# Four graph layers on one core: another order of the middle layers' work, X0's numbers on GpSimd, the last sums tile by tile

## The chip, the core and the metric

The kernel runs on one core of a Trainium2 chip. The time is that of one execution on the device in microseconds (us), the median of several runs. Engines are called as in the profile: PE (TensorE matmul), PEld (its weight load), DVE (VectorE), ACT (ScalarE), POOL (GpSimd), SP (SyncE, which issues the DMAs here).

## The reference

`x` is 3327 x 64, `adj` a 3327 x 3327 matrix of zeros and ones (about 0.5% ones). Four layers follow each other, each on the normalized input:

```python
h = jnp.maximum(_layernorm(x, axis=-1), 0.0)
x = x + layer(h, adj, ...)          # layers 0, 1, 2, 3

# layers 0 and 3, hyperbolic attention (layer 3 with c = 1 / r**2)
left, right = x_tan @ att_W[:D] + att_b, x_tan @ att_W[D:]      # x_tan = logmap0(x)
adj_att = sigmoid(left + right.T) * adj
x_local = logmap(x[:, None, :], x[None, :, :], C)
support_t = einsum('ij,ijd->id', adj_att, x_local)
return proj(expmap(x, support_t, C), C)

# layer 1, decay by rank among a row's neighbours
mask = (adj != 0); rank = cumsum(mask, axis=1); deg = rank[:, -1:]
k = minimum(deg, 100); pos = rank - (deg - k)
w = mask * where(pos > 0, 0.5 ** (k - pos), 0)
return w @ (h @ weight) + bias

# layer 2, sums over neighbours without the diagonal, and GRU cells
node_support = concat([(A > 0) @ h, (A < 0) @ h], axis=1)       # A = adj - its diagonal
edge_output = gru_cell(node_support, h, ...)
edge_support = softmax attention of A, times A, @ (h @ W_gat)
node_output = gru_cell(edge_support, h, ...)
return d[:, None] * edge_output + d[:, None] * node_output      # d = diagonal of adj
```

## The kernel before, in words

The nodes are padded to 3328, which is T = 26 tiles of 128 (P). The features D are 64. `X` holds all nodes as 128 x 26 x 64 in SBUF; half of it is 128 x 832 elements (`HALVES`).

**Hyperbolic layers (0 and 3).** A preparation (from L395) computes per node the factors that the pairwise logarithm needs. Its parts bear on the change: `of_x0` (L454), seven DVE operations of 128x26 that compute `x0` and split it into three fp16 parts; `of_e` (L463) and `of_f` (L467), which lay these parts out in the fp16 tile `Xe`; `to_columns16` (L478), which transposes 26 tiles of `Xp` or `Xe` by PE into PSUM tiles of four and has ACT and DVE in turn copy them out as XT and XE; `keep_busy` (L494), matmuls whose result nobody reads, 4 (L499) and 6 (L531); `of_left` (L514), which spreads `left` over the partitions; and small per-node numbers (L538 to L544). The operations on ACT, DVE, PE and POOL stand here in the order in which the code writes them. Then 104 steps follow (four chunks of columns, 1024 or 768 wide, by 26 tiles of rows). A step has two matmul pairs on PE (L588, L589), a Sigmoid on ACT (L575), a product with adjacency on POOL (L577), a Square on ACT (L595), two passes on DVE (L600, L601) and sums on PE (L610, L618). An epilogue (L698 to L796) computes per-node factors `ah` and `am` in some 60 operations of 128x26 and adds `ah * Xr + am * M` to X: per half of X a product (L793) and a sum (L794) for each of the two terms, where for the last term ACT has already made the product (`extra`, L786). This epilogue is not ordered by hand; a scheduler places its operations.

**Layer 1, decay** (`plain_decay`, L1273). The adjacency is read in 52 quarter tiles of 128x1664. For each, DVE makes an fp8 mask (L1326, 128x1664) and counts its zeros (`same`, L1248), PE counts ranks by triangular matrices (L1333), ACT turns them into weights by Exp (L1339), and PE sums (L1350). Its own layernorm (`norm_relu`, L123 to L146) and the product with the weight stand after the first two masks and ahead of the loop (L1386 to L1426). For 13 of the 52 quarters (`LATE`) the count of zeros is put off to layer 2.

**Layer 2, GAT** (`plain_gat`, L1431). PE sums over the masks kept from layer 1, in 26 steps (`b` from 25 to 0, L1518) of 16 matmuls each. In every second step DVE does one of the 13 late zero counts, for which the adjacency quarter is loaded again into a pool of 3 buffers (L1451). A table `todo` (L1510) puts other work behind certain steps: the transposes of h (`turn`), the degrees less the diagonal (`degrees`, L1488) and their inverse (`inverse`, L1497). After the steps `take` (L1536 to L1539) brings the sums from PSUM by ACT (L1538) and DVE (L1539), and two GRU cells follow in eight units: products on PE (L1546 to L1558), gates on ACT (L1565), `nn` on DVE (L1571, L1572), Tanh on ACT (L1575), the state on DVE (L1582 to L1586), and at the end the sum into X (L1613, L1614).

In the manually ordered pools, engine queues keep the order of the code. ACT has function tables: `table_of(F)` (L119) uses a function once on a spare element, so that its table is loaded at that place.

Of the kernel before, what the change touches and what calls it, by code (L numbers as in the profile page):

```python
# [9 lines left out]
F32 = mybir.dt.float32  # L10
# [36 lines left out]
def tile_gnn4(ctx: ExitStack, tc: tile.TileContext, x, adjT, att0, b0, w1, bias1, w_gat, a_gat,  # L47
# [274 lines left out]
    def hyperbolic_series(r, params, ok, masks=None, done=None):  # L322
# [18 lines left out]
        with ExitStack() as st:  # L341
# [53 lines left out]
            with tc.tile_pool(name="hsp", bufs=1) as tp, tc.tile_pool(name="hsps", bufs=2, space=PSUM) as ps, \  # L395
                    tc.manual_schedule(engines={mybir.EngineType.Activation, mybir.EngineType.DVE,
                                                mybir.EngineType.PE, mybir.EngineType.Pool}):
                Xe = tp.tile([P, T, KE + 9], F16, name="Xe")
# [11 lines left out]
                H, R, sq, sr = [tp.tile([P, T, D], F32, name=n) for n in ("H", "R", "sq", "sr")]  # L410
# [43 lines left out]
                def of_x0():  # L454
                    V.scalar_tensor_tensor(x0, x2, 1.0, ia, op0=OP.add, op1=OP.mult)
                    V.tensor_scalar(x0s, x0, SX, None, op0=OP.mult)
                    V.tensor_copy(p0[:, :, 0], x0s)
                    V.tensor_sub(rest, x0s, p0[:, :, 0])
                    V.tensor_copy(p0[:, :, 1], rest)
                    V.tensor_sub(rest, rest, p0[:, :, 1])  # L460
                    V.tensor_copy(p0[:, :, 2], rest)

                def of_e():  # L463
                    for k, src in ((0, h0.to_broadcast([P, T, 3])), (3, m0.to_broadcast([P, T, 2])), (5, l0)):
                        V.tensor_copy(E[:, :, k:k + src.shape[-1]], src)

                def of_f():  # L467
                    for k, src in ((0, p0), (3, hm0), (5, h0)):
                        V.tensor_scalar(Fe[:, :, k:k + src.shape[-1]], src, -1.0, None, op0=OP.mult)
                    G.tensor_copy(F, Fe)  # L470
# [7 lines left out]
                def to_columns16(dst, src, rows, odd, between=()):  # L478
                    between = list(between)
                    for t0 in range(0, T, 4):  # L480
                        n = min(4, T - t0)
                        pt = ps.tile([P, 4 * P], F16, name="pt", bufs=4)
                        for k in range(n):
                            PE.transpose(pt[:rows, k * P:(k + 1) * P], src[:, t0 + k, :], ident_h)  # L484
                        if t0 // 4 % 2 == odd:
                            V.tensor_copy(dst[:, t0 * P:(t0 + n) * P], pt[:rows, :n * P])
                        else:
                            A.activation(dst[:, t0 * P:(t0 + n) * P], pt[:rows, :n * P], AF.Copy)
                        if between:
                            between.pop(0)()  # L490

                junk, pe = [ps.tile([P, W], F32, name=n, bufs=1) for n in ("junk", "pe")]

                def keep_busy(n):  # L494

                    for _ in range(n):
                        PE.matmul(junk, ident_h, hi[:, :8, :], start=True, stop=True)

                keep_busy(4)  # L499
                to_columns16(XT, Xp[:, :, :2 * D], P, 1,  # L500
                             (of_x0, of_e, of_f, lambda: V.tensor_copy(Xe[:, :, :D], hi), of_z))
                columns(chunks[0])

# [8 lines left out]
                c = chunks[0]  # L512

                def of_left():  # L514

                    for o, to in ((0, junk), (1, pe)):
                        for i in range(c[1]):
                            t = o * HT + c[0] + i
                            PE.matmul(to[:, i * P:(i + 1) * P], left[:, t:t + 1].to_broadcast([P, P]), ident,
                                      start=True, stop=True)  # L520
                    V.tensor_copy(leftB[c][:, 0, :], junk[:, :c[1] * P])
                    A.activation(leftB[c][:, 1, :], pe[:, :c[1] * P], AF.Copy)

                to_columns16(XE, Xe, KE + 9, 0, (lambda: None, of_left))
                for o in range(2):
                    pt = ps.tile([P, 4 * P], F16, name="pt", bufs=4)
                    for i in range(c[1]):
                        PE.transpose(pt[:KE, i * P:(i + 1) * P], Xp[:, o * HT + c[0] + i, D:], ident_h)
                    V.tensor_copy(XF[c][:, o, :], pt[:KE, :c[1] * P])
                PE.transpose(pe[:T, :P], left, ident)  # L530
                keep_busy(6)  # L531
                A.activation(LT, pe[:T, :P], AF.Copy)
                nc.sync.dma_start(left_row, LT)
                V.tensor_copy(X0[:, :, 0], x0)
                V.scalar_tensor_tensor(good, x2, X2_MIN, nodes, op0=OP.is_ge, op1=OP.mult)
                V.reduce_sum(ok, good, axis=AX.X)
# [7 lines left out]
                V.tensor_scalar(small["bh"], ax, 0.5, isqc, op0=OP.mult, op1=OP.mult)  # L544

# [143 lines left out]
            with tc.tile_pool(name="hse", bufs=1) as tp:  # L689
# [43 lines left out]
                else:  # L733
# [8 lines left out]
                    V.tensor_mul(th, th, ti)  # L742
# [44 lines left out]
                for ts in HALVES:  # L787
                    for a, b in ((Xr, ah), (M, am)):
                        if ts is last and a is M:
                            prod = extra  # L790
                        else:
                            prod = tp.tile([P, T // 2, D], F32, name="prod", bufs=2)
                            V.tensor_mul(prod, a[:, ts, :], b[:, ts, None].to_broadcast([P, T // 2, D]))  # L793
                        V.tensor_add(X[:, ts, :], X[:, ts, :], prod)  # L794
                    if done is not None:
                        done(ts)  # L796
# [476 lines left out]
    def plain_decay(masks, zo, deg, wt, bias, gru, ball_of_r):  # L1273
# [11 lines left out]
        with ExitStack() as st:  # L1285
# [24 lines left out]
            with tc.tile_pool(name="pdacc", bufs=1, space=PSUM) as pa, tc.manual_schedule(  # L1310
# [20 lines left out]
                def counts(k, o, w):  # L1331
                    for h in range(2):
                        PE.matmul(cnt[o][:, h, :BK], w, cols(k, o, h), start=w is after and steps[k][1] == T - 1,  # L1333
                                  stop=True, skip_group_check=True)
# [30 lines left out]

                K_ = len(steps)
                make_mask(0)
                make_mask(1)
# [15 lines left out]
                for o in range(2):  # L1384
                    cnt[o] = pa.tile([P, 2, 512], F32, name=f"cnt{o}")
                for k in range(K_ + 2):  # L1386
                    c, b = steps[min(max(k, 0), K_ - 1)]
                    if 0 <= k < K_:
                        counts(k, 0, after)
                        weights(k, 0)  # L1390
                    if 0 <= k - 1 < K_:
                        counts(k - 1, 1, rest)
                        if steps[k - 1][1] == 0:
                            degrees(steps[k - 1][0], 1)
                    if 0 <= k < K_:
                        counts(k, 1, after)
                        weights(k, 1)
# [4 lines left out]
                    if 0 <= k < K_:  # L1402
                        counts(k, 0, rest)
                        if b == 0:
                            degrees(c, 0)
# [4 lines left out]
                    if k == 1:  # L1410
                        late()
# [19 lines left out]
    def plain_gat(masks, zo, deg, first, wg, gru):  # L1431
# [8 lines left out]
        with ExitStack() as st:  # L1440
# [10 lines left out]
            wk = st.enter_context(tc.tile_pool(name="pgl", bufs=3))  # L1451
# [4 lines left out]
            with tc.tile_pool(name="pgp", bufs=1) as tp, tc.tile_pool(name="pgacc", bufs=1, space=PSUM) as pa, \  # L1456
# [4 lines left out]

                hn = tp.tile([P, T, D], F32, name="hn")
# [25 lines left out]
                def degrees(k):  # L1488

                    cs = slice(k * BK, (k + 1) * BK)  # L1490
                    dg = bank(6 + k % 2)[:, :BK]
                    for o in range(2):
                        PE.matmul(dg[o * D:(o + 1) * D, :], ones_bf[:, :D],
                                  diag[:, o * HP + k * BK:o * HP + (k + 1) * BK], start=True, stop=True)
                    V.tensor_sub(deg[:, cs], deg[:, cs], dg)

                def inverse():  # L1497
# [8 lines left out]
                    table_of(AF.Sigmoid, r0[:, :1])  # L1506
                    V.scalar_tensor_tensor(deg, deg, -1.0, r0, op0=OP.mult, op1=OP.mult)
                    V.scalar_tensor_tensor(deg, deg, 2.0, r0, op0=OP.add, op1=OP.mult)

                todo = {T - 4: lambda: turn(0), T - 6: lambda: degrees(0), T - 8: lambda: turn(4),  # L1510
                        T - 9: lambda: degrees(1), T - 11: lambda: turn(8), T - 12: lambda: degrees(2),
                        T - 14: lambda: turn(12), T - 15: lambda: degrees(3), T - 17: inverse}
                for b in range(T - 1, -1, -1):
# [9 lines left out]
                    if b % 2 == 0:  # L1523
                        same = wk.tile([P, 2, CW], BF, name="same", bufs=1)
                        k = LATE[(T - 1 - b) // 2]
                        zeros(same, late.pop(0), zo[:, k:k + 1])


# [173 lines left out]
```

## Time and profile before

| | us |
|---|---|
| median of 3 runs (lowest, highest) | 819.15 (817.87, 821.02) |
| profiled execution, its time | 818.34 |
| its span | 816.6 |

The mean granted clock of PE was 0.924 in it. Busy share of the span: DVE 87%, PE 81%, ACT 71%, POOL 51%. The stages in the trace, from the span's start, are:

| stage | from, to (us) |
|---|---|
| layer 0: preparation; loop; epilogue | 0 to 36; 36 to 266; 267 to 284 |
| layer 1: norm; loop | 284 to 298; 298 to 428 |
| layer 2: norm; loop over masks; GRU cells and sum | 428 to 443; 443 to 486; 486 to 531 |
| layer 3: preparation; loop; epilogue | 531 to 561; 561 to 790; 791 to 811 |

In a line of a timeline the columns are: start, duration, engine, line of the code, operation, output and input by their names and shapes, count, and in square brackets the idle time just before on this engine and what ended it. "x2" with 2.08 us is two instructions in a row. Starts of successive lines can lie closer than the duration of one: operations overlap on an engine, and their pitch is what a sum needs. In a line of windows the numbers after the length are busy times of PE, PEld, DVE, ACT and POOL with counts, the mean clock, the DMA share and GB/s.

### The profile page before, as it was taken

What the parts mean: (1) busy time and instruction counts of PE and PEld (TensorE: products, weight loads), DVE (VectorE), ACT (ScalarE), POOL (GpSimd) and SP (SyncE); (2) the same over time, 40 slices, a digit from 0 to 9 for tenths busy, and PEclk for the clock granted to TensorE, in tenths of its full rate; (3) what the DMA queues carried; (4) which work ended last, traced back from release to release, by engine and by line L of the source; (5) the groups of instructions that cost most, each with busy time, mean ns of one, the idle gap of its engine ahead of it and who ended that gap; (6) DMA issues with size and microseconds to landing.
All of it is one profiled execution on the core that took longest, in us unless ns stands there. A gap on an engine that the chain in (4) does not pass through costs nothing. (4 is left out here: it accounts for less than half of the span.)

```text
span 816.6 us, 11802 instructions
## 1 busy us (share of the span) xinstructions
PE 659.8 (81%) x4215; PEld 252.1 (31%) x4215; DVE 709.1 (87%) x985; ACT 576.2 (71%) x729; POOL 416.1 (51%) x296
## 2 busy tenths in 40 slices
PE   0799999999999049989993995427999999999960
PEld 0522233333332024435441651214222333333320
DVE  6789999989998899998967567996899999999976
ACT  2678888878886367777782575255888888888862
POOL 2299988989987050003120000004687777787730
PEclk9989999999999569999996997757999999999995
DMA  3567676776664739998913541001001001000001
GB/s 75 164 203 219 205 212 184 205 213 196 196 189 120 292 131 327 372 379 298 367 36 132 187 151 50 1 4 45 1 1 34 1 1 36 1 1 2 1 2 46
DMA packets 57621, 107.84 MB, mean 132 GB/s; under 512 B 8752, under 2 KB 33488, under 8 KB 57552
## 3 DMA queue, kind: packets, MB, share of 16 engines
q1 hardware_dynamic: 53200, 106.97, 40.5%
q10 hardware_dynamic: 4352, 0.02, 0.3%
q8 instruction: 35, 0.57, 0.3%
q14 instruction: 34, 0.28, 0.1%
HBM read 103.72 MB, written 0.88 MB: 128 GB/s over the span
## 5 line engine op out<-in xcount | busy, mean ns | idle before, releaser
L595 ACT ACTIVATE y<-slot,shift_c 128x768 f32<-128x768 f32 (+1 forms) x208 | 197.4, 949 | 68.4 <-ACT sig L575 48.6
L601 DVE TENSOR_TENSOR sig<-slot,sig 128x768 f32<-128x768 f32 (+1 forms) x208 | 213.2, 1025 | 23.3 <-POOL sig L577 2.1
L600 DVE SCALAR_TENSOR_TENSOR slot<-y,slot 128x768 f32<-128x768 f32 (+1 forms) x208 | 212.1, 1020 | 9.1 <-ACT y L595 9.0
L577 POOL TENSOR_TENSOR sig<-adj,sig 128x768 f32<-128x768 f32 (+1 forms) x104 | 201.9, 1962 | 28.1 <-ACT sig L575 26.0
L575 ACT ACTIVATE sig<-leftB,right 128x768 f32<-128x768 f32 (+1 forms) x208 | 204.1, 981 | 3.5 <-DVE bh L544 3.5
L577 POOL TENSOR_TENSOR sig<-mask,sig 128x768 f32<-128x768 fp8e4 (+1 forms) x104 | 174.6, 1680 | 61.6 <-ACT sig L575 57.6
L610 PE MATMUL slot<-sig,Xr 128*64 128x384 f32 (+1 forms) x832 | 188.3, 541 | 16.8 <-DVE sig L601 16.8
L588 PE MATMUL slot<-XC,XT 128*128 128x384 f16 (+1 forms) x416 | 142.9, 344 | 5.2 <-DVE sig L601 3.5
L589 PE MATMUL slot<-XF,XE 73*128 73x384 f16 (+1 forms) x416 | 142.0, 341 | 0.0
L1339 ACT ACTIVATE w<-cnt,ebias 128x832 bf16<-128x832 f32 x104 | 93.7, 950 | 30.7 <-PE cnt L1333 30.7
L1248 DVE TENSOR_SCALAR_CACHE_REDUCE same<-adj 128x1664 bf16<-128x1664 f32 x52 | 97.5, 1876 | 3.6 <-DMA adj<-in 3.4
L618 PE MATMUL slot<-sig,X 128*32 128x384 f32 (+1 forms) x832 | 96.0, 533 | 0.0
L610 PEld LDWEIGHTS slot<-sig,Xr 128*64 128x64 f32 x832 | 43.1, 135 | 122.5 <-DVE sig L601 83.4
L1333 PE MATMUL cnt<-mask,after 128*128 128x416 fp8e4 x208 | 54.8, 347 | 22.7 <-DVE mask L1326 19.8
L588 PEld LDWEIGHTS <-XT 128*128 128x128 f16 x416 | 40.8, 98 | 96.1 <-issue 70.7
L191 POOL TENSOR_TENSOR mask<-mask,offdiag 128x128 fp8e4<-128x128 fp8e4 x26 | 15.0, 594 | 97.9 <-PE cnt L1333 97.9
L1333 PE MATMUL cnt<-mask,rest 128*128 128x416 fp8e4 x208 | 54.7, 345 | 10.2 <-ACT w L1339 10.2
L400 POOL MEMSET X<- 128x832 f32 x2 | 1.6, 794 | 115.0 <-PE pt L1234 115.0
L1326 DVE TENSOR_SCALAR mask<-adj 128x1664 fp8e4<-128x1664 f32 x52 | 52.9, 1035 | 0.0
L589 PEld LDWEIGHTS <-XE 73*128 73x128 f16 x416 | 40.9, 98 | 33.6 <-issue 9.9
L1350 PE MATMUL acc<-w,h 128*64 128x416 bf16 x416 | 46.6, 345 | 0.0
L1518 PE MATMUL bank<-mask,h 128*64 128x416 fp8e4 x416 | 39.7, 348 | 0.0
(299 smaller groups left out, 521.8 us busy)
## 6 DMA issues: line engine op xcount, KB each, us to landing
adj<-in SPq DMA_DIRECT2D x65, 832.0 KB, 6.6
adj<-in SPq DMA_DIRECT2D x78, 384.0 KB, 3.9
adj<-in SPq DMA_DIRECT2D x27, 512.0 KB, 4.4
leftB<-left SPq DMA_DIRECT2D x6, 384.0 KB, 3.5
XC<-XT SPq DMA_DIRECT2D x12, 96.0 KB, 4.3
X<-in SPq DMA_DIRECT2D x2, 416.0 KB
out<-X SPq DMA_DIRECT2D x2, 416.0 KB, 2.4
XF<-XT SPq DMA_DIRECT2D x6, 96.0 KB, 2.6
```

Source lines behind the costliest of these rows:

```text
L575: A.activation(sig, leftB[c], AF.Sigmoid, bias=right[:, b:b + 1])
L577: G.tensor_tensor(sig, adj, sig, op=OP.mult)
L588: PE.matmul(L[:, o, :c[1] * P], XT[:, rows], XC[c][:, o, :], start=True, stop=False)
L589: PE.matmul(L[:, o, :c[1] * P], XE[:KE, rows], XF[c][:, o, :], start=False, stop=True)
L595: A.activation(ys[k], Ls[k][:, :, :c[1] * P], AF.Square, scale=-0.5 / SX ** 2, bias=shift_c)
L600: V.scalar_tensor_tensor(L, y, G3, L, op0=OP.add, op1=OP.mult)
L601: V.tensor_mul(sig, L, sig)
L610: PE.matmul(acc[c][o * D:(o + 1) * D, 0, :n], Xr[:, b, :], sigs[k][:, o, :], start=b == 0, stop=b == T - 1)
L618: PE.matmul(acc[c][q:q + 32, 1, :n], X0[:, b - 1 + i, :], w[:, o, :], start=b == 1, stop=b == T - 1, tile_position=(0, q))
L1248: V.tensor_scalar(same, adj, 0.0, 0.0, op0=OP.is_equal, op1=OP.add, accum_out=count)
L1333: PE.matmul(cnt[o][:, h, :BK], w, cols(k, o, h), start=w is after and steps[k][1] == T - 1, stop=True, skip_group_check=True)
L1339: A.activation(ws[k][:, o, :, :], cnt[o][:, :, :BK], AF.Exp, scale=-LN2, bias=ebias)
```

## The change

It touches four places.

In the preparation of both hyperbolic layers, the numbers of X0, E and F are computed by POOL (15 operations) instead of DVE (13 and a copy on POOL). The two groups of dummy matmuls shrink to one of two. ACT copies out the first three groups of XE and DVE the other four, where they took turns. LT is copied by DVE, and the small per-node numbers move earlier on DVE.

```diff
                 def of_x0():
-                    V.scalar_tensor_tensor(x0, x2, 1.0, ia, op0=OP.add, op1=OP.mult)
-                    V.tensor_scalar(x0s, x0, SX, None, op0=OP.mult)
...
+                    G.tensor_scalar(x0, x2, 1.0, None, op0=OP.add)
+                    G.tensor_tensor(x0, x0, ia, op=OP.mult)
+                    G.tensor_scalar(x0s, x0, SX, None, op0=OP.mult)
...
-                keep_busy(4)
-                to_columns16(XT, Xp[:, :, :2 * D], P, 1,
-                             (of_x0, of_e, of_f, lambda: V.tensor_copy(Xe[:, :, :D], hi), of_z))
+                of_x0()
+
+                for _ in range(2):
+                    PE.matmul(junk, ident_h, hi[:, :8, :], start=True, stop=True)
+                groups = range(0, T, 4)
+                for t0 in groups:
+                    to_columns16(XT, Xp[:, :, :2 * D], P, t0, (A, V)[t0 // 4 % 2])
...
-                keep_busy(6)
-                A.activation(LT, pe[:T, :P], AF.Copy)
...
+                for t0 in groups[:3]:
+                    to_columns16(XE, Xe, KE + 9, t0, A)
...
+                for t0 in groups[3:]:
+                    to_columns16(XE, Xe, KE + 9, t0, V)
```

In the epilogue of both, the product `th` is written to a tile of its own, and six of the wide operations on halves of X become 39 operations on one tile of 128x64 each, with the factor as a scalar by partition:

```diff
-                    V.tensor_mul(th, th, ti)
+                    ta, th = th, new("th_t")
+                    V.tensor_mul(th, ta, ti)
...
                         if ts is last and a is M:
-                            prod = extra
+                            V.tensor_add(X[:, ts, :], X[:, ts, :], extra)
                         else:
-                            prod = tp.tile([P, T // 2, D], F32, name="prod", bufs=2)
-                            V.tensor_mul(prod, a[:, ts, :], b[:, ts, None].to_broadcast([P, T // 2, D]))
-                        V.tensor_add(X[:, ts, :], X[:, ts, :], prod)
+                            for t in range(ts.start, ts.stop):
+                                stt(X[:, t, :], a[:, t, :], b[:, t:t + 1], X[:, t, :], op0=OP.mult, op1=OP.add)
```

In layer 1 the counts and weights of the first two quarters stand ahead of the norm, with the table of Exp asked for first and that of Sqrt after them:

```diff
-                make_mask(0)
-                make_mask(1)
+                table_of(AF.Exp)
...
+                for k in range(2):
+                    make_mask(k)
+                    counts_before(k)
+                    counts(k, 0, rest)
+                table_of(AF.Sqrt)
                 H = pers.tile([P, T, D], F32, name="H")
```

In layer 2 the late zero counts stand in batches, the pool of loaded quarters has 4 buffers, and the other work behind the steps is moved earlier or together:

```diff
-            wk = st.enter_context(tc.tile_pool(name="pgl", bufs=3))
+            wk = st.enter_context(tc.tile_pool(name="pgl", bufs=4))
...
                     table_of(AF.Sigmoid, r0[:, :1])
+                    check(4)
                     V.scalar_tensor_tensor(deg, deg, -1.0, r0, op0=OP.mult, op1=OP.mult)
                     V.scalar_tensor_tensor(deg, deg, 2.0, r0, op0=OP.add, op1=OP.mult)
-
-                todo = {T - 4: lambda: turn(0), T - 6: lambda: degrees(0), T - 8: lambda: turn(4),
-                        T - 9: lambda: degrees(1), T - 11: lambda: turn(8), T - 12: lambda: degrees(2),
-                        T - 14: lambda: turn(12), T - 15: lambda: degrees(3), T - 17: inverse}
+                    check(len(late))
+
+
+                todo = {T - 2: lambda: check(4), T - 4: lambda: turn(0), T - 6: lambda: degrees(0, 1),
+                        T - 7: lambda: check(3), T - 8: lambda: turn(4), T - 10: lambda: degrees(2, 3),
+                        T - 11: inverse, T - 12: lambda: turn(8), T - 15: lambda: turn(12)}
...
-                    if b % 2 == 0:
-                        same = wk.tile([P, 2, CW], BF, name="same", bufs=1)
-                        k = LATE[(T - 1 - b) // 2]
-                        zeros(same, late.pop(0), zo[:, k:k + 1])
```

## Prediction

> **What bounds the kernel now.** I read the table of windows, cut at the stages, then the timeline of each stage in which an engine is well under full, then the chain of waits.
>
> ```profile
> 36.00:267.00 231.00, 218.56 (x1268) 68.69 (x1266) 210.06 (x221) 190.20 (x223) 208.32 (x112) 0.99 0.66 192
> 267.00:284.00 17.00, 0.00 (x0) 0.00 (x0) 15.16 (x63) 5.78 (x18) 0.00 (x0) 0.56 0.83 319
> 284.00:298.00 14.00, 2.75 (x8) 1.14 (x9) 12.44 (x18) 6.09 (x8) 7.76 (x16) 0.50 0.44 161
> 298.00:428.00 130.00, 124.41 (x845) 57.22 (x843) 120.31 (x132) 99.31 (x116) 18.33 (x32) 0.99 0.79 285
> 486.00:504.00 18.00, 8.00 (x47) 2.31 (x43) 12.94 (x20) 9.43 (x18) 0.00 (x0) 0.72 0.27 95
> ```
>
> Columns: the stretch, its length, then busy time of PE, its weight loads, DVE, ACT and POOL, the clock, DMA share, GB/s. The two hyperbolic loops (this one, and 561 to 791) and the decay loop hold PE at 95 to 96% and DVE at 91 to 93%. The change leaves the inner order of all three alone, so 590 of the 816.6 us of span can only shift. What can move are the seams. One is plainly slack: 486 to 504, the end of the GAT layer's loop over masks. PE has 8 of 18 us to do, and DVE's 12.9 are mostly the wrong work:
>
> ```profile
> 484.53 1.88 DVE L1248 TENSOR_SCALAR_CACHE_REDUCE same<-adj 128x1664 bf16<-128x1664 f32 x1
> ...
> 491.37 1.89 DVE L1248 TENSOR_SCALAR_CACHE_REDUCE same<-adj 128x1664 bf16<-128x1664 f32 x1 [1.10 <-DMA adj<-in]
> ...
> 495.61 1.89 DVE L1248 TENSOR_SCALAR_CACHE_REDUCE same<-adj 128x1664 bf16<-128x1664 f32 x1 [2.35 <-DMA adj<-in]
> ...
> 497.43 1.58 DVE L1539 SCALAR_TENSOR_TENSOR deg<-bank,deg 128x416 f32<-128x416 f32 x3
> ```
>
> ```profile
> 498.16 3.04 PE L1553 MATMUL bank<-xh,gw 128*64 128x416 f32 x8 [10.00 <-DVE deg L1539]
> ```
>
> PE's last mask product ends at 485.07. DVE's takes of it (L1539) wait behind five zero checks, which themselves wait twice for adjacency tiles still in flight (3 buffers). PE stands 10 us for the takes.
>
> **GAT: checks in batches, 4 buffers.** The number of checks is the same (13 of 1.88). They now sit behind mask steps T-2, T-7 and in `inverse`, all before the take in DVE's order. DVE had 24.0 us of work in the 43 us from 443 to 486; five checks more (9.4) make 33.4, which fits, if the loads come. A load took about 7 us from issue to landing near 488; with a fourth buffer and all issues behind checks that are done earlier, I put the last check at about 479. Then takes 0 and 1 start when PE ends (485.1 plus 0.6 us, as between the product and ACT's first use). Takes 2 and 3 of DVE's half stand behind ACT's L1538 ones, which end at 490.05 and 491.1 in the trace, since ACT first loads Sigmoid's table (1.28 at 486.73). So the second product's inputs are ready at 491.7 rather than 499.6, and the gates (ACT L1565, 503.39 before) come at about 495.0: **-8.3** (7 to 9). What is late next is ACT: takes, table load, gates. The new interleaving of `o` and X sums at the layer's end lets DVE fill gaps between gates; 26.03 of 27 us are busy there: **-0.5** (-1 to 0).
>
> **Decay: two steps' counts ahead of the norm.** On PE these are fourteen count matmuls (eight stood there before), on ACT four Exp of 0.95, all now ahead of the norm's Square. And Sqrt's table must come back after them.
>
> ```profile
> 288.97 1.83 ACT L135 ACTIVATE ln_sq<-H 128x832 f32<-128x832 f32 x2 [9.13 <-DVE H L134]
> 292.11 0.23 ACT L98 ACTIVATE ln_sd<-ln_v 128x26 f32<-128x26 f32 x1 [1.30 <-DVE ln_v L138]
> 292.35 1.28 ACT L119 ACT_TABLE_LOAD   x1
> ```
>
> The 9.13 us wait looks like free room for them. It isn't quite: mask 0 is there at 285, PE is at clock 0.50 and takes 0.35 us a count matmul, and with mask 1 two us later the four Exp end at about 290.6. The Sqrt load and its spare (1.28 + 0.20) end at 292.1, where Square began at 288.97: 3.2 late. DVE, at 12.44 of 14 us here, waits for Square and has nothing queued before it but the norm. POOL's bias work meets less of DVE's, about -0.5. **+2.7** (2.0 to 3.5). What does the loop give back? PE waits for DVE's masks until 314.18 (four waits of 0.19 to 0.24 there), so counts done early only lengthen those waits; DVE is busy without a gap from 298.1 on but for 2.91 us, and its work is the same. I take **0**; the bound on the gain side is the moved PE work with the two Exp pairs' latency, about 4 us.
>
> **Epilogues: six wide operations become 39 narrow ones.** The trace before has no 64-element operation with a scalar pointer; near rows are these.
>
> ```profile
> 801.52 0.23 DVE L775 TENSOR_SCALAR am<-am,isqc 128x26 f32<-128x26 f32 x1
> 801.66 0.23 DVE L776 TENSOR_SCALAR n<-n,maxn 128x26 f32<-128x26 f32 x1
> ...
> 803.73 1.03 DVE L793 TENSOR_TENSOR prod<-Xr,ah 128x832 f32<-128x832 f32 x1
> 804.67 1.02 DVE L793 TENSOR_TENSOR prod<-M,am 128x832 f32<-128x832 f32 x1
> 805.61 2.08 DVE L794 TENSOR_TENSOR X<-X,prod 128x832 f32<-128x832 f32 x2
> ```
>
> Two 26-element pointer operations start 0.14 apart; with 38 more elements at the wide rows' slope (0.94 between starts for 832 elements, and 0.10 for 26, gives about 1.05 ns an element) one takes 0.18 to 0.19. Sum: 39 x 0.187 = 7.3, plus the `extra` sum that stays (1.02), is 8.4 with a start, against 803.73 to 810.80 = 7.07 before. **+1.3 each, +2.6.** Bounds: at 0.14 each, -0.5; at 0.28, each operation's whole duration paid in turn, +4.9. Here a rule speaks against the change: the Trainium skill, "VectorE: DVE Perf Modes", section "The TRN2 errata — SBUF-src ops pay a fixed extra latency per instruction", puts a fixed term of some 150 cycles and 8 of fill on every operation between SBUF tiles and says to keep tiles at 512 or more. By it an operation costs (158 + 64) / 0.96 GHz = 231 ns, the sum is 39 x 0.231 = 9.0, and an estimate from that page is +3 per epilogue. The rows show a pitch of 0.14 although each lasts 0.23, so the fixed part overlaps with the next operation; I go by the rows. Second, in the last epilogue `th` no longer is written over, and this wait goes:
>
> ```profile
> 798.50 0.19 DVE L742 TENSOR_TENSOR th<-th,ti 128x26 f32<-128x26 f32 x1 [1.46 <-ACT spare L119]
> ```
>
> **-1.4**, since the DVE chain behind it is dependent to the end. Next late is DVE itself.
>
> **Preparation.** X0's numbers leave DVE: 13 operations, 2.4 us, for 15 on POOL, which at POOL's rows (0.19 to 0.26 for 26 elements, 0.41 for 128x234) last 4.5 us from 18.05. Their reader is the XE transpose at 26.7, so 4 us of slack hide them. If that cover were gone, each us late would be a us. Beside POOL work DVE's L143 took 1.25 rather than 1.03, so I charge +0.2 each. The dummy matmuls (eight fewer) had no reader. In the third layer's preparation DVE and ACT then end at 558.6 instead of 560.25, and the first sig follows: **-1.5** with the contention. In the first one, the built program shows another thing: the decay layer's `table_of(AF.Exp)`, which depends on nothing, is placed among ACT's XT evictions. It costs 1.5 us there (0.9 after slack), and throws out Sigmoid's table, so 1.28 us of load now stand in front of the first sig. First sig at about 35.7, not 35.15: **+0.75** with contention.
>
> **Sum.** 0.75 + 1.3 + 2.7 + 0 - 8.3 - 0.5 - 1.5 + (1.3 - 1.4) = -5.65. The profiled execution took 818.34 (span 816.6 and 1.7 around it), so 812.7; the median of three runs, 819.15, is 0.8 above it, which gives **813.5**.
>
> **Rivals.**
> *Counts pay in full.* If PE is the bound of the decay loop from its start, each count done early shortens it, about 4 us: 809.5. For it: PE is 124.4 of 130 busy, and masks cost it only 0.9 us of waits. Against it: those waits stand early, and a lighter PE only meets the same mask later.
> *The take's wait is replaced.* The checks in `inverse` come last; if their tiles land late, or ACT's takes are the chain, half of 8.3 is lost: 817.7. For it: ACT's part of the chain is known only from a stretch in which it waited. Against it: the DMA engines are lightly used here (share 0.27, 95 GB/s), so a load that is issued early has no reason to land late.
> *Slower: PE cold at the loop starts.* The dummy matmuls and the six at the end kept PE's window filled; without them both loops may start at half clock and stay there. The trace has the clock at 0.5 from 42 to 46 and 567 to 573 even with them. "TensorE: Matmul & The Clock Gate" (the Trainium skill, Part 1) asks for a busy window of about 3.4 us to get the full clock and one idle window to lose it. At half clock (eight L618 products took 1.94 us there) I estimate PE at about 3.8 us per 1024-wide tile where DVE takes 2.45: 1.35 us lost per tile. From about two more cold tiles per loop on, the gain is eaten; with four, 813.5 + 2 x 4 x 1.35 = 824.3. Against it: loop work is dense, so it warms the array by itself within a tile or two, as it does now.
>
> **How the numbers follow.** The sum 0.56 (own range 811 to 816); counts pay in full 0.20, 809.5; wait replaced 0.16, 817.7; cold loops 0.08, 824.3. A measurement of this kernel can tell about 0.5% (4.1 us), so faster means below 815.05. Of the main case some 0.46 of 0.56 lies below that, with all of the 0.20: 0.66. Slower means above 823.2, most of the cold case: 0.07. Same: 0.27. The range 808.5 to 818.5 takes in the first three cases and the bounds of the epilogues' price.
>
> **What would show it.** Right: DVE's last zero check before 482, L1539 within 1 us of PE's last mask product, PE's 10.00 wait gone; Square of the decay norm near 292; 39 operations at a pitch near 0.19; a Sigmoid load just ahead of the first sig. Wrong: decay's last product less than 2.7 us later relative to its start (counts paid), a DMA wait in front of a zero check after 482, or granted clock under 0.9 in the loops' second 10 us.

## The result, and the profile after

The changed kernel takes 813.03 us (811.81 to 814.64, 5 runs), the kernel before beside it 819.15 (817.03 to 821.02, 5 runs): a ratio of 0.9923, 95% interval 0.9904 to 0.9942. The forecast was 813.5. The profiled execution took 812.35, with a span of 810.2.

One total can hide errors that cancel, so the sum was checked at marks that both traces have. The table gives the start of an operation in each, how far the changed kernel is ahead (-) or behind (+) at it, and what was added since the mark above it.

| mark | before | after | shift | since last mark | forecast |
|---|---|---|---|---|---|
| first sig, layer 0 | 35.15 | 36.07 | +0.92 | +0.92 | +0.75 |
| last sums of the loop, layer 0 | 263.84 | 264.99 | +1.15 | +0.23 | 0 |
| first mask, layer 1 | 283.85 | 286.76 | +2.91 | +1.76 | +1.3 |
| normalized H, first half | 293.72 | 299.89 | +6.17 | +3.26 | +2.7 |
| first mask product, layer 2 | 443.63 | 449.17 | +5.54 | -0.63 | 0 |
| first Tanh, layer 2 | 501.74 | 498.67 | -3.07 | -8.61 | -8.3 |
| first sum of layer 3 (L413) | 531.13 | 527.57 | -3.56 | -0.49 | -0.5 |
| first sig, layer 3 | 560.37 | 554.47 | -5.90 | -2.34 | -1.5 |
| last sums of the loop, layer 3 | 788.60 | 782.00 | -6.60 | -0.70 | 0 |
| first last-sum of X | 803.73 | 795.77 | -7.96 | -1.36 | -1.4 |
| the `extra` sum | 809.78 | 803.60 | -6.18 | +1.78 | +1.3 |

So one part pays for all, and half of the others cost. The part that pays, in the timelines of DVE and PE of the changed kernel (columns as before; the GAT layer begins 5.54 later here):

```profile
480.46 1.88 DVE L1243 TENSOR_SCALAR_CACHE_REDUCE same<-adj 128x1664 bf16<-128x1664 f32 x1
...
482.38 1.89 DVE L1243 TENSOR_SCALAR_CACHE_REDUCE same<-adj 128x1664 bf16<-128x1664 f32 x1
...
491.20 0.59 DVE L1562 SCALAR_TENSOR_TENSOR deg<-bank,deg 128x416 f32<-128x416 f32 x1 [6.68 <-ACT xh L1561]
...
495.61 0.59 DVE L1562 SCALAR_TENSOR_TENSOR deg<-bank,deg 128x416 f32<-128x416 f32 x1 [2.75 <-ACT xh L1561]
```

```profile
497.32 0.93 PE L1581 MATMUL bank<-xh,gw 64*64 64x416 f32 x8 [2.08 <-DVE deg L1562]
```

The last check ends at 484.27 (478.73 when the 5.54 are taken off), and DVE then stands idle for 6.68 us before the first take. The takes no longer wait for checks, but for ACT's copies, the first of which waits for PE's last mask sums. PE's wait of 10.00 is 2.08. The next two blocks show what is paid. First ACT ahead of the decay layer's norm: four Exp and a Sqrt load in front of Square, which starts at 294.84.

```profile
289.04 1.80 ACT L1334 ACTIVATE w<-cnt,ebias 128x832 bf16<-128x832 f32 x2 [6.75 <-PE cnt L1328]
291.63 1.80 ACT L1334 ACTIVATE w<-cnt,ebias 128x832 bf16<-128x832 f32 x2 [0.79 <-PE cnt L1328]
293.44 1.28 ACT L119 ACT_TABLE_LOAD   x1
...
294.84 1.67 ACT L135 ACTIVATE ln_sq<-H 128x832 f32<-128x832 f32 x2
```

Then the last sums of X in the first epilogue on DVE. Thirteen narrow operations start 2.56 us before the next thirteen (277.87 to 280.43), so one costs 0.197:

```profile
277.87 2.64 DVE L789 SCALAR_TENSOR_TENSOR X<-Xr,ah,X 128x64 f32<-128x64 f32 x13
280.43 2.63 DVE L789 SCALAR_TENSOR_TENSOR X<-M,am,X 128x64 f32<-128x64 f32 x13
...
285.70 1.02 DVE L786 TENSOR_TENSOR X<-X,extra 128x832 f32<-128x832 f32 x1
```

And in the first preparation ACT loads Sigmoid's table again, behind the last DVE operation:

```profile
34.77 1.28 ACT L569 ACT_TABLE_LOAD   x1 [2.55 <-DVE ok L538]
36.07 1.15 ACT L569 ACTIVATE sig<-leftB,right 128x1024 f32<-128x1024 f32 x1
```

### The profile page after: what moved, and what is told of

It reads as the page before. It is cut to its first block, busy times and chain, and to the rows that moved or that the text cites. A ratio compares the mean times of both kernels' runs of the same rounds, so it can differ in the third digit from the quotient of the medians.

```text
span 810.2 us, 11836 instructions
## 1 busy us (share of the span) xinstructions
PE 656.8 (81%) x4199; PEld 252.2 (31%) x4199; DVE 709.2 (88%) x1027; ACT 580.5 (72%) x733; POOL 426.3 (53%) x324
```

## The experiments

In this section "ratio" is a kernel's time by that of the kernel before on the same chip, with its 95% interval. The kernel before had medians of 819.15 to 821.71 on the chips used, so differences between kernels of different chips are taken from ratios, at 820 us.

### The GAT layer alone, and which half of it

`gat_only` is the kernel before with only the GAT function of the change.

> The kernel before with the change's GAT layer alone. Theory (the zero checks, moved ahead of the takes, free the takes): 8.6 us less for the loop's end and 0.5 for the last sums, 819.15 - 9.1 = 810.0. Rival (the change's gain comes from the other parts, and the wait re-forms behind ACT's takes): half of it, about 814.8.

Measured: 810.05 (809.51 to 812.54), ratio 0.9888 (0.9870 to 0.9905). The theory holds: this part alone is worth 9.2 us, more than the whole change (6.3). In its profile the stretch from the first mask product to the first Tanh is 8.9 us shorter than before.

`gat_3buf` takes the fourth buffer away again:

```diff
-            wk = st.enter_context(tc.tile_pool(name="pgl", bufs=4))
+            wk = st.enter_context(tc.tile_pool(name="pgl", bufs=3))
```

> As the kernel before with the GAT layer alone, but with 3 buffers for the quarters that are loaded again, not 4. Theory (where the checks stand decides): within 1 us of that kernel, about 810.5, with short DMA waits in front of a few checks. Rival (the fourth buffer decides): the last checks wait for their loads as before, and half of the gain or more is lost, 814.5 to 819.

Measured: 810.94 (809.68 to 813.04), ratio 0.9894 (0.9875 to 0.9913). The theory holds. DMA waits in front of checks come back, five of 2.9 us in all, but at places where DVE has time to spare: it still stands idle for 5.40 us between the last check and the first take. In the view of waits (us in total, times, longest):

```profile
DVE same L1248 <- DMA adj<-in: 2.9, 5, 1.3
```

`gat_spread4` has 4 buffers, but a check in every second step and the old table of other work:

```diff
-                todo = {T - 2: lambda: check(4), T - 4: lambda: turn(0), T - 6: lambda: degrees(0, 1),
...
+                todo = {T - 4: lambda: turn(0), T - 6: lambda: degrees(0), T - 8: lambda: turn(4),
...
+                    if b % 2 == 0:
+                        check()
```

> As the kernel before with the GAT layer alone, with 4 buffers, but one check behind every second step and the other work at its old steps. Theory (where the checks stand decides): five checks of 1.9 us still stand between the inverse and the takes; only their DMA waits, 1.10 and 2.35 us, go: about 815.7. Rival (the fourth buffer decides): about 810.5.

Measured: 816.63 (815.47 to 818.88), ratio 0.9960 (0.9947 to 0.9973). The theory holds here too. The trace of this kernel shows the five checks back to back without a DMA wait, and the takes behind them at 494.77; PE waits 6.63 where it waited 10.00:

```profile
492.96 1.89 DVE L1248 TENSOR_SCALAR_CACHE_REDUCE same<-adj 128x1664 bf16<-128x1664 f32 x1
...
494.77 1.08 DVE L1552 SCALAR_TENSOR_TENSOR deg<-bank,deg 128x416 f32<-128x416 f32 x2
```

```profile
495.50 2.95 PE L1566 MATMUL bank<-xh,gw 128*64 128x416 f32 x8 [6.63 <-DVE deg L1552]
```

So the order decides, and what the buffer is worth depends on it. In the old order the fourth buffer alone is worth 3.3 us, about the two DMA waits of 1.10 and 2.35 that go. In the new order 3 buffers already give 8.7 us, and the fourth adds 0.5, which the intervals don't tell from nothing: the same 13 checks stand where DVE was waiting anyway.

### The last sums

`wide_sums` is the changed kernel with the six wide operations (the `th_t` tile stays):

```diff
-                            V.tensor_add(X[:, ts, :], X[:, ts, :], extra)
+                            prod = extra
                         else:
-                            for t in range(ts.start, ts.stop):
-                                stt(X[:, t, :], a[:, t, :], b[:, t:t + 1], X[:, t, :], op0=OP.mult, op1=OP.add)
+                            prod = tp.tile([P, T // 2, D], F32, name="prod", bufs=2)
+                            V.tensor_mul(prod, a[:, ts, :], b[:, ts, None].to_broadcast([P, T // 2, D]))
+                        V.tensor_add(X[:, ts, :], X[:, ts, :], prod)
```

> The changed kernel with the last sums of X as six wide operations again (the new th tile stays). Theory (a narrow operation costs its pitch, 0.197 us in the changed kernel's trace): 1.77 us less in each of the two epilogues, 813.03 - 3.5 = 809.5. Rival by the fixed term of a page, 0.231 us each: 2.9 less each, 807.2. Rival (the narrow ones are hidden in the first epilogue, since DVE waits for the masks' loads after it anyway): 1.8 less in all, 811.3.

Measured: 810.22 (809.59 to 812.13), ratio 0.9885 (0.9866 to 0.9904), 3.1 us less than the changed kernel. That is nearest to the theory, and too little for the 0.231 us of the page named in the prediction. With an interval of some 2 us either way the total can't exclude the second rival, 1.8 in all, but the marks of the profile do: 1.78 less in the first epilogue and 1.77 in the last. Each is 39 x 0.197 and 0.15 more ahead of the `extra` sum, against 6.06 for six wide ones. The narrow operations are a loss, in the first epilogue too.

### The decay layer and the early table

`decay_undone` is the changed kernel with the decay function of before (norm first, counts in the loop).

> The changed kernel with the decay layer as before: norm first, counts of the first two quarters in the loop. Theory: Square and what follows it 3.3 us earlier, the loop 0.6 longer, and with the early request of Exp's table gone from the first preparation about 2.5 less there (no Sigmoid load before the first sig, 1.28, and no late XT copies): 813.03 - 5.2 = 807.8. Rival (the counts ahead of the norm do shorten the loop, and what was lost lies elsewhere): 811 to 814.

Measured: 809.84 (808.33 to 810.61), ratio 0.9876 (0.9856 to 0.9897), 3.9 us less. The theory has the sign and part of the size. Its marks: first sig 2.33 earlier, the norm 3.26 shorter, and the loop with its end 2.08 longer. Of these 2.08 only 0.63 are expected. The trace has PE's clock at 0.50 from 362.3 to 365.7, in the middle of the loop, which the changed kernel's trace has not; the other 1.45 are put down to that, and the last experiment returns to it.

`no_exp_table` takes out the request alone:

```diff
-                table_of(AF.Exp)
-
                 def counts_before(k):
```

> The changed kernel without the early request of Exp's table in the decay layer; Exp is then loaded by itself in front of its first use. Theory (the request is placed in the first preparation and throws Sigmoid's table out there): the first sig comes 2 to 2.6 us earlier, the rest is unchanged: 810.7. Rival (only the visible Sigmoid load counts): 1.3 less, 811.7. Rival (the request hid a load that now stands on the path to the first weights): 813.

Measured: 812.88 (811.38 to 815.55), ratio 0.9920 (0.9898 to 0.9942): no difference from the changed kernel that the intervals show. In its profile both loads are gone from the first preparation and the first sig comes at 33.38 (2.69 earlier, of which 0.3 is an earlier start), yet 1.2 of that is lost within layer 3's loop, and the span is 809.2, 1.0 less. More profiles settle the size: the first sig stands at 33.38 to 33.82 in five profiles of kernels without the request, and at 34.82 to 36.07 in three with it (the changed kernel, `wide_sums`, `sqrt_tied`), so the request costs about 1.7 us at that mark. In the total of this one kernel it isn't to be seen, within intervals of some 1.5 us. Nor does the request save anything later: layer 0's Sigmoid throws Exp's table out again, and ACT loads it once more ahead of the first weights, at 281.00 with the request and at 278.58 without.

### The preparation

`prep_only` is the kernel before with the changed preparation alone.

> The kernel before with the preparation of both hyperbolic layers as changed, and nothing else; so no request of Exp's table falls into the first one. Theory (the preparation is bound by DVE's chain): the first sig comes 1.4 us earlier in layer 0 and 2.3 in layer 3, 819.5 - 3.7 = 815.8. Rival (with fewer dummy matmuls the loops start at a lower clock and give this back): 818 to 820.

Measured: 815.48 (813.16 to 816.66), ratio 0.9938 (0.9917 to 0.9960), 5.1 us less. The theory holds: first sig 1.33 earlier in layer 0, and layer 3's preparation 3.67 shorter in this profile, 5.0 together. The rival is out.

`x0_on_vector` is the changed kernel with `G.` written as `V.` in `of_x0`, so that all 15 operations stand on DVE ahead of the XT copies.

> The changed kernel with X0's numbers, E and F on DVE, at the place where the change starts them on GpSimd. Theory (GpSimd hides them): 15 operations, about 2.4 us of DVE time, stand ahead of the XT copies in each preparation: 2.4 more twice, 817.8. Rival (GpSimd's sharing of DVE's port costs as much as it hides): within 1 us, 813 to 814.

Measured: 815.76 (814.97 to 816.86), ratio 0.9951 (0.9932 to 0.9970), 2.3 more than the changed kernel. The total lies between the two, with an interval of some 2 us either way. The marks are nearer to the theory: the first sig comes 1.39 later and layer 3's preparation is 2.59 longer, together 4.0 of the 4.8 expected. So the move to GpSimd is worth 2 to 4 us for both layers, a large part of the preparation's 5.1; the rest is left to the new order, which no run tried by itself.

`dummies_back` restores the matmuls that nobody reads:

```diff
-                for _ in range(2):
+                for _ in range(4):
                     PE.matmul(junk, ident_h, hi[:, :8, :], start=True, stop=True)
...
                 PE.transpose(junk[:T, :P], left, ident)
+                for _ in range(6):
+                    PE.matmul(pe, ident_h, hi[:, :8, :], start=True, stop=True)
```

> The changed kernel with 4 dummy matmuls ahead of the XT transposes and 6 after the last transpose, as before. Theory (the loops' start is not decided by them): within 1 us of 813.0, and the stall of ACT and PE near the loops' fifth tile goes back from 2.6 to about 3.6 us if they had any part in it. Rival (they kept the clock up): the tiles at the loop's start run faster and 1 to 3 us are gained, 810 to 812.

Measured: 813.92 (812.82 to 815.77), ratio 0.9932 (0.9911 to 0.9953). Within 1 us of 813, so the rival with cold loops is out. Its profile has the first sig 1.71 earlier in layer 0 and 0.48 later, by its own part, in layer 3; the total shows neither. ACT's stall near the fifth tile of layer 3, 3.62 us in the kernel before and 2.57 in the changed one, is 2.50 with the dummies back, so they had no part in it.

### Where a request of a table ends up

Reading the GAT layer's timeline of ACT in both kernels showed that the load ahead of the first gates, which the prediction took as given, is made by the kernel itself: layer 3's `table_of(AF.Sqrt)`, which depends on nothing, is placed ahead of the takes. It throws out Sigmoid's table, requested just before, and the table comes back behind the first takes (ACT of the changed kernel):

```profile
476.71 1.28 ACT L119 ACT_TABLE_LOAD   x1
478.00 0.20 ACT L119 ACTIVATE spare<-ln_sq 128x1 f32<-128x1 f32 x1
...
482.68 1.28 ACT L119 ACT_TABLE_LOAD   x1
483.97 0.20 ACT L119 ACTIVATE spare<-one_c 128x1 f32<-128x1 f32 x1
490.12 2.13 ACT L1561 ACTIVATE xh<-bank 64x416 f32<-64x416 f32 x4 [5.94 <-PE bank L1543]
492.26 1.28 ACT L1588 ACT_TABLE_LOAD   x1
```

The load at 476.71 is Sigmoid's, asked for with a value of the inverse as operand (`ln_sq`); the one at 482.68 is Sqrt's, asked for with a constant (`one_c`). `sqrt_tied` ties the second one:

```diff
-                table_of(AF.Sqrt)
+                if r is None:
+                    table_of(AF.Sqrt)
...
                     if 0 <= u - 1 < K:
                         tanh(u - 1)
+                        if u - 1 == K - 1:
+                            table_of(AF.Sqrt, gates[u - 1][1][:, :1])
```

> The changed kernel with one edit in a place that the change left alone: layer 3's early request of Sqrt's table, which both traces show in front of the takes, is tied to the last gate of the GAT layer. Theory (that request throws Sigmoid's table out, so 1.28 us of load stand between the takes and the first gates): 1.3 less at the gates, up to 0.7 less at layer 3's first Sqrt, 813.0 - 1.8 = 811.2. Rival (the takes' chain on DVE hides the load): within 0.5 of 813.0.

Measured: 810.43 (809.53 to 811.44), ratio 0.9886 (0.9866 to 0.9905), 3.0 us less than the changed kernel, with intervals that take in the 1.8. The first gate now follows the takes at once, on ACT:

```profile
490.66 2.12 ACT L1562 ACTIVATE xh<-bank 64x416 f32<-64x416 f32 x4 [7.48 <-PE bank L1544]
492.80 1.21 ACT L1589 ACTIVATE gate<-bank,gs 128x416 f32<-128x416 f32 x2
493.91 2.08 ACT L1562 ACTIVATE xh<-bank 64x416 f32<-64x416 f32 x4
```

By the marks the stretch from mask product to Tanh is 1.19 us shorter; layer 3's preparation gains nothing (27.01 against 26.90). The theory holds for the first half only; the rest of the 3.0 isn't accounted for by it.

### The parts put together

`best` is the changed kernel with `wide_sums`, `decay_undone` and `sqrt_tied` together.

> The changed kernel with wide last sums, the decay layer as before and layer 3's table request tied. Theory (the parts add up): wide sums 3.1 to 3.5 less, decay 3.3 to 4.0 less, the table 1.8 less: 813.0 - 8.6 = 804.4. Rival (the parts overlap, above all at the loops' starts): 807 or more.

Measured: 804.04 (802.70 to 807.25), ratio 0.9805 (0.9783 to 0.9828). The parts add up. It is 16 us faster than the kernel before, and about 9.7 faster than the change.

Its profiled execution was the slowest of its five, at 807.25, and the trace shows where. From H of the norm to the first mask product it took 154.23 us, where the kernel before took 149.91 with the same decay code. In the windows of `best` the figure behind the five engines' busy times is PE's clock:

```profile
348.00:362.00 14.00, 11.12 (x72) 4.76 (x69) 14.00 (x17) 10.25 (x14) 0.00 (x0) 0.94 1.01 375
361.00:367.00 6.00, 5.73 (x22) 2.04 (x23) 6.00 (x9) 3.47 (x7) 0.41 (x1) 0.50 1.03 404
```

It falls to 0.50 in the middle of a dense loop. In the timeline, just ahead of it, PE waits twice for ACT's copies of the degrees (1.04 and 1.85 us), and after it the same eight sums take 1.60 instead of 0.89:

```profile
358.56 0.51 PE L1329 MATMUL cnt<-mask,after 128*128 128x416 fp8e4 x2 [1.04 <-ACT deg L1351]
...
361.27 0.85 PE L1329 MATMUL cnt<-mask,after 128*128 128x416 fp8e4 x2 [1.85 <-ACT deg L1351]
362.06 1.60 PE L1346 MATMUL acc<-w,h 128*64 128x416 bf16 x8
```

The kernel before has the same two waits (1.04 and 1.84) with the clock at 1.00 throughout. `best_filled` gives PE something to do there:

```diff
+                def fill(n, h):
+                    for _ in range(n):
+                        PE.matmul(filled[h], parts[0][:, :2, :], masks[12][:, 1, :BK], start=True, stop=True)
...
+                    if k == T:
+                        filled.extend(pa.tile([P, BK], F32, name=f"acc{h}", bufs=2) for h in range(2))
+                        fill(5, 0)
...
+                    if k == T:
+                        fill(9, 1)
                     if 0 <= k < K_:
                         counts(k, 1, after)
```

> The faster version (wide last sums, decay as before, table request tied) with 14 matmuls whose result nobody reads, 5 and 9, in the two pauses of PE at the middle of the decay loop, where it waits 1.04 and 1.85 us for ACT's degree copies. They go to the accumulator that the next sums start anew. Theory (that pause lets the clock fall in some executions, for up to 6.9 us and at a cost of 0, 1.5 or 3 us by its phase): the clock stays at 1.00 there, H of the norm to the first mask product of the GAT layer takes 150 us instead of 154, and the median falls by 1 to 3 us, 801 to 803. Rival (the fall of the clock there doesn't come from the pause, or costs nothing): 804, with rows of the same length.

Measured: 803.73 (802.57 to 803.94), ratio 0.9797 (0.9768 to 0.9827). In this profile the two waits are 0.16 and 0.26 us, the clock stays at 1.00 and the stretch takes 149.91 us:

```profile
360.00:364.00 4.00, 3.74 (x25) 1.75 (x24) 4.00 (x5) 3.36 (x7) 0.00 (x0) 1.00 0.97 372
```

The median is the same as that of `best` within the interval, so the 1 to 3 us that the theory gave it are not there; the five runs lie within 1.4 us of each other instead of 4.6. Five runs of each are few for a spread, so the totals are consistent with the theory and don't prove it.

The other profiles say more. All thirteen kernels without the fill have the two pauses, of 1.04 and 1.84 or 1.85 us. In nine of their profiles the clock is at 0.50 there, for 3.4 us in eight and for 6.8 in `best`; the fall begins between 0.8 us ahead of the end of the second pause and 1.5 us behind it. In the other four (the kernel before, the changed one, `no_exp_table`, `x0_on_vector`) it stays at 1.00. Between 311 and 425 us no profile has a fall at any other place. In `gat_only`, for one, it lasts from 361.7 to 365.1:

```profile
362.00:365.00 3.00, 2.75 (x12) 0.89 (x12) 3.00 (x4) 1.89 (x4) 0.00 (x0) 0.50 1.03 414
```

So a fall behind these pauses is the common case. With the old decay code the stretch takes 149.91 us without one and 151.20 to 151.49 with one of 3.4 us, in four profiles; in `prep_only`, whose loop also starts cold for longer, it takes 153.02. Since four of thirteen profiles are clean without the fill, the one clean profile with it is weak evidence that the fill is the cure. It also means that marks on two sides of this loop can differ by 1.4 us between two profiles whatever was changed.

## Why the prediction was right

The total was right, and not by cancelling alone: seven of eleven marks lie within 0.5 us of their forecast, and all within 0.85. Some luck is in it, since the errors of the marks, +1.95 and -2.48 us, add up to -0.53.

Two parts put in alone give -9.2 us (GAT) and -5.1 (preparations); two taken out of the change show that they cost +3.1 (sums) and +3.9 (decay with its early request). With -1.4 for the `th` tile, which no run tried by itself, this makes -8.7, where the whole change is -6.3. Each of the four has an interval of 1.4 to 2.3 us either way, so the totals don't close the sum more closely than that; the marks do.

*The takes behind the checks.* -8.61 in the trace, -8.9 when tried alone, against -8.3. What was called late next is late next: ACT's takes and the Sigmoid load, in front of the first gates. The rival in which half of it is lost is out. The fourth buffer, which the sum gave part of the credit, has little of it in this order: 3 buffers lose 0.5 us of 9.2. The sign "last check before 482" was set in the time of the kernel before, where the check ends at 478.73.

*Decay.* The norm came 3.26 later instead of 2.7: Square is 2.96 late (3.2 worked out), and the norm behind it took 0.30 longer where GpSimd was to give back 0.5. (Ahead of the norm the trace before has four count matmuls, not eight; eight is the count of the whole window from 284 to 298.) The loop gave back 0.63 where 0 was forecast, so the sign "less than 2.7 later relative to its start" was met, with 2.63. That is the rival "counts pay in full" at a sixth of its size. The reason against it fits: PE's waits for masks in the loop went up from 0.9 us to 1.4.

*Narrow sums.* The step that was mis-sized is the pitch: 0.187 was taken, 0.197 is measured, which is 0.4 of the 0.5 between 1.77 and 1.3 an epilogue. The rule of "VectorE: DVE Perf Modes" (the Trainium skill), with 0.231 us, was further off, by 0.034 an operation. (Its section on the errata counts the fill into the 150 cycles; that gives 0.223, still too much.) By that page's own 0.96 GHz, 64 elements are 0.067 us, so the fixed part here is an estimated 0.130 us, or 125 cycles and not some 150, for operations that stand in a row without waiting for each other.

*Preparations.* Here the step was mis-sized, in both layers the same way. Layer 3's stretch, from L413 to the first sig, took 25.57 to 27.18 us in eight profiles with the changed preparation, and 29.01 to 30.09 in four with the old one: some 2.9 less on the mean, where 1.5 was forecast. In layer 0 the changed preparation with the early table request brings the first sig at 34.82 to 36.07, against 35.15 to 35.75 with the old one: about equal, not 0.75 later. That a table request without a dependency travels, and lands in the first preparation, is there in the trace (a load at 23.69, between ACT's copies of XT). The 0.2 us charged for GpSimd's contention with DVE don't show: DVE's L442 and L446 beside GpSimd take 1.97 and 2.00 us for two, 1.96 and 1.97 before. It is GpSimd that is slowed, as the last section shows.

*Cold loops*, the rival on the other side, did not come: the loops' own lengths changed by +0.23 and -0.70. The sign set for it, a clock under 0.9 in a loop's second 10 us, was met in layer 0 (0.83 from 46.07 to 56.07; 0.98 in layer 3), but the kernel before meets it too, with 0.89 and 0.87, so it could not tell the two apart.

## What to carry to other kernels

Before a wait is blamed on memory alone, look at what the waiting engine does in between: five checks that nobody needed yet stood in front of four takes that everybody waited for, and moving them was worth more than all else. A request of an ACT table is an instruction without inputs, and goes wherever the scheduler has room: tie it to a value that is ready just before the table is needed. Splitting a wide DVE operation into narrow ones to save a pass is paid by the fixed part: here two wide passes of 13 x 64 elements, about 1.0 us each (6.06 for six), beat 13 fused ones at 0.197.

## What the runs showed of the hardware

Small GpSimd operations slow down beside wide DVE operations with two inputs. In the changed kernel's first preparation these lines of POOL, the first four of which run beside DVE's L442 and L446 (18.27 to 22.27), take about four times what the same kinds take just after (L459 beside L461, L460 beside L462). "GPSIMD Engine Reference" of the Trainium skill, section Specifications, says that the SBUF interfaces are shared with DVE and that DVE operations with two SBUF inputs contend; the size is this trace's, and the last line is the same L461 in layer 3, beside DVE's L446 there:

```profile
18.49 0.96 POOL L457 TENSOR_SCALAR x0s<-x 128x26 f32<-128x26 f32 x1
19.52 0.80 POOL L458 CAST p<-x0s 128x26 f16<-128x26 f32 x1
20.41 0.97 POOL L459 TENSOR_TENSOR rest<-x0s,p 128x26 f32<-128x26 f32 x1
21.45 0.91 POOL L460 CAST p<-rest 128x26 f16<-128x26 f32 x1
22.44 0.25 POOL L461 TENSOR_TENSOR rest<-rest,p 128x26 f32<-128x26 f32 x1
22.75 0.23 POOL L462 CAST p<-rest 128x26 f16<-128x26 f32 x1
...
542.49 0.88 POOL L461 TENSOR_TENSOR rest<-rest,p 128x26 f32<-128x26 f32 x1
```

One operation thus takes 0.25 us in layer 0 and 0.88 in layer 3, by what stands beside it; the traces of all nine kernels with these operations on GpSimd show the same. So X0's numbers ended at 25.20, not 22.6 as 4.5 us of POOL work from 18.05 would have it, and 1.4 us of the 4 us of slack ahead of the transposes at 26.60 was left.

And two pauses of PE of 1.04 and 1.85 us, with less than a microsecond of products between them, were followed by half the clock in nine of thirteen profiles, for 3.4 us in eight and for 6.8 in `best` (360.5 to 367.3). The Trainium skill, "TensorE: Matmul & The Clock Gate", Part 1, speaks of one idle window of about 3.4 us; neither pause is as long. The totals of two kernels can't tell such a loss from one that a change makes; the row with the clock beside it can. Why it falls in some executions and not in others, with the same pauses, is not settled by these runs.
